# A graph network on one core: the opening of its first stage is put in another order, and its products get a wider ring of accumulators

## The chip, the cores and the metric

The kernel runs on one core of a Trainium2 chip. The metric is the device time of one execution in microseconds. It is compared by the median of several runs. The profile is that of a single further execution, so its own time stands beside its span below.

## What is computed

Four graph layers over the same 2708 nodes of 512 features, each with a residual and a layer norm. The change touches the first of them only. Cut to what matters:

```
keep    = (adj > 0) & (cumsum(adj > 0, axis=1) <= 64)     # the first 64 neighbours of a row
nb_mean = (keep @ x) / max(keep.sum(1), 1)
xj      = leaky_relu(nb_mean @ W_nb.T + b_nb)
xi      = leaky_relu(x @ W_line.T + b_line)
x       = layernorm(x + xi + where(cnt > 0, xj, 0))
# then three more layers of the form x = layernorm(x + layer(x, adj, ...))
```

The other layers are a mean over all neighbours, an attention with 8 heads, and a two-stage attention with a two-layer network behind it.

## The kernel before

The nodes are cut into 22 tiles of 128 rows (`NT`), the last of 20 rows. The features are 4 blocks of 128 (`KD`). A product of a tile with a 512 x 512 weight is four logical matmuls in float32; the trace shows each as two instructions of TensorE.

The first stage (lines 329 to 425) runs over the tiles of `x` and does three things side by side.

- **Two products per tile.** Tile `t` is fetched on SP's queue (line 175), transposed by TensorE in four pieces (line 134) into a PSUM tile `ps_tr`, and copied to `xT` by ScalarE (line 136). Then it is multiplied by `wnT` (line 397; for tiles 0 and 1 line 344) and by `wlT` (line 415). The first result is split by `keep_y` into a rounded part `yH` (ScalarE, line 241) and a rest `yL` (VectorE, line 246). The second gets its bias on VectorE, as `u` (line 417), and goes to DRAM on GpSimd's queue (line 418).
- **Counts of 14 masks** (`HERE`). A mask is 128 rows of the adjacency matrix, loaded and converted to bf16 on GpSimd's queue (line 282) into one of three tiles `m`. `count` (line 287, ScalarE) makes 0 and 1 of it and sums each row. `place` (lines 293 and 296, VectorE) marks, by a scan along the row and a product, which neighbours are among the first 64; it is done in two halves, one before and one after `u` in the program.
- **Turning of the masks.** Each is transposed into `maskT`, one way or the other. Some go through a DMA transpose on SP's queue (line 314) and are written by ScalarE two tiles later (`signs`, line 319). The others go through 22 transposes on TensorE (line 305), in three groups that take an accumulator each and are written by ScalarE (line 309).

[...]two tiles `ps_tr`, one each of `pm0` and `pm1` (pool `ps_mm`, for products with `wnT` and `wlT`), and a ring of four tiles `acc` (pool `ps_a`, handed out by `sums()`). Products with `wnT` use `acc` in odd tiles and `pm0` in even ones; products with `wlT` always use `pm1`; the groups of turned masks use `acc`.

Ahead of the loop stand the weights. `transpose_weight` (lines 139 to 148) fetches a weight in four strips, transposes each with TensorE and copies it with VectorE. In the kernel before, `wnT` is made, then tiles 0 and 1 are multiplied by it, then `wlT` is made, then the loop begins. The first two mask tiles get their zero padding from VectorE once `wlT` is done (line 354); later ones from GpSimd (line 356).

The order of the work comes from the program, from a planner that lays out each engine's queue when the kernel is built, and from ties written out by hand. `pe(...)` chains TensorE instructions in the order in which they are written. `tc.issue_after(ins)` puts what is written inside it behind `ins` on the same engine. `early(first, n, make)` makes tiles `first` steps ahead of their use. Which tile counts a mask is decided by `now` (line 406): in tile `t` one is counted if fewer than `(t - 1) * 14 / 17`, rounded up, have been.

The second stage (from line 429) multiplies the turned masks with `yH` and `yL` (line 573) and processes the other eight masks meanwhile.

Of the kernel before, what the change touches and what calls it, by code (L numbers as in the profile page):

```python
# [19 lines left out]
P = 128  # L20
D = 512
KD = D // P
# [9 lines left out]
def kernel(  # L32
# [9 lines left out]
    nc = tc.nc  # L42
    N = x.shape[0]
    NT = -(-N // P)
# [17 lines left out]
    ident = const.tile([P, P], F32, name="ident")  # L62
# [4 lines left out]
    ones = const.tile([P, P], F32, name="ones")  # L67
# [37 lines left out]
    def pe(ins):  # L105

        for i in ins.ins if isinstance(ins.ins, tuple) else (ins.ins,):
            if behind:
                tc.add_manual_dep(i, behind[0], mybir.DependencyInfo(
                    mybir.DependencyClass.NoSync, mybir.DependencyReason.DATA), reason="order")  # L110
            behind[:] = [i.name]
# [4 lines left out]
    def layer_norm(pool, y, n, dst, on_scalar=False):  # L116
# [10 lines left out]
        nc.vector.scalar_tensor_tensor(mv[:n, 0:1], mv[:n, 0:1], -1.0, rs[:n], op0=OP.mult, op1=OP.mult)  # L127
        nc.scalar.activation(dst, y, AF.Identity, bias=mv[:n, 0:1], scale=rs[:n])

    def transposed(pool, psum, src, n, name, order=as_it_comes):  # L130

        ps = psum.tile([P, KD, P], F32, name="ps_tr")
        for k in range(KD):
            order(nc.tensor.transpose(ps[:, k, :n], src[:, k * P:(k + 1) * P], ident[:n, :n]))
        dst = pool.tile([P, KD, P], F32, name=name)
        nc.scalar.copy(dst[:, :, :n], ps[:, :, :n])  # L136
        return dst

    def transpose_weight(room, psum, dst, src, queues=(nc.sync,)):

        for ki in range(KD):
            wr = room[ki]
            queues[ki % len(queues)].dma_start(wr, src[ki * P:(ki + 1) * P, :])
            ps = psum.tile([P, KD, P], F32, name="ps_tr")
            for ko in range(KD):
                pe(nc.tensor.transpose(ps[:, ko, :], wr[:, ko * P:(ko + 1) * P], ident))
            made = nc.vector.tensor_copy(dst[:, :, ki * P:(ki + 1) * P], ps)
        return made


    fast = ctx.enter_context(ExitStack())
# [55 lines left out]
    with ExitStack() as phase:  # L207
# [30 lines left out]
        highs = {}  # L238

        def keep_y(t, n, pm):  # L240
            highs[t] = nc.scalar.copy(yH(t)[:n], pm[:n])
            if t == LAST:
                low = slice(TWIN, TWIN + n)
                nc.scalar.copy(yL(t)[low], pm[low])
                return nc.vector.tensor_sub(yH(t)[low], pm[low], yL(t)[low].bitcast(F32))
            return nc.vector.tensor_sub(yL(t)[:n], pm[:n], yH(t)[:n].bitcast(F32))
# [5 lines left out]
        def product(xT, n, w, which, order=as_it_comes, pm=None):  # L252
            pm = ps_mm.tile([P, D], F32, name=f"pm{which}") if pm is None else pm
            if n == few and order is as_it_comes:
                nc.gpsimd.memset(xT[:, :, n:32], 0.0)
                for k in range(KD):
                    nc.tensor.matmul(pm[32 * k:32 * k + 32], xT[:, k, :32], w[:, k, :], start=True, stop=True)
                u = sm.tile([P, D], F32, name="u")
                nc.scalar.copy(u, pm)
                pm = sums()  # L260
                nc.tensor.matmul(pm[:TWIN + few], groups4[:, :TWIN + few], u, start=True, stop=True)
                return pm
            m = n
            if n == few:
                m = TWIN + n
                nc.gpsimd.memset(xT[:, :, n:TWIN], 0.0)
                nc.gpsimd.tensor_copy(xT[:, :, TWIN:m], xT[:, :, :n])
            for k in range(KD):
                order(nc.tensor.matmul(pm[:m], xT[:, k, :m], w[:, k, :], start=(k == 0), stop=(k == KD - 1)))  # L269
            return pm  # L270
# [58 lines left out]
        with ExitStack() as ph:  # L329
            st = ph.enter_context(tc.tile_pool(name="l0a", bufs=1))  # L330
            wnT, wlT = weight(), weight2
            room = [maskT[:, G + k, :4 * D].bitcast(F32) for k in range(2 * KD)]

            fetches = []
            xs = early(2, NT, lambda t: fetched(x, t, rows(t), log=fetches))
            xTs = early(0, NT, lambda t, order=as_it_comes: transposed(ahead, ps_tr, xs(t), rows(t), "xT", order))

            transpose_weight(room[:KD], ps_tr, wnT, l0_w_nb, (nc.sync, nc.scalar))  # L340
            lows = {}
            for t in range(2):
                xT = xTs(t, order=pe)
                lows[t] = keep_y(t, P, product(xT, P, wnT, 0, pe))
            weights_made = transpose_weight(room[KD:], ps_tr, wlT, l0_w_line)
            b_line = bias(bcast(l0_b_line, D))
            def mask_tile():
                return st.tile([P, NT * P], BF16, name="m", bufs=3)

            def mask_rows(i):  # L350
                m = mask_tile()
                if i < 2:
                    with tc.issue_after(weights_made.ins):
                        nc.vector.memset(m[:, (0 if rows(turns[i]) < P else N - 1):], 0.0)
                else:
                    nc.gpsimd.memset(m[:, N:], 0.0)
                return load_mask(i, m)

            def by_dma(i):
                return i % 2 == 0 and i < HERE - 2  # L360

            def turned_tile():
                return end_tile(BF16)[:, :NT * P].rearrange("p (t n) -> p t n", n=P)

            masks = early(1, HERE, mask_rows)
            intos = {}

            def turn_next(i):
                if not by_dma(i):
                    for _ in turn_here(i, masks(i), lambda: sums(BF16, (P, G, P)), pe):  # L370
                        pass
                    return
                assert len(intos) < 2
                intos[i] = turned_tile()
                with tc.issue_after(fetches[-1].ins):
                    turn(i, masks(i), intos[i])
                due.append((t + 2, i))

            def signs_of(i, t):
                with tc.issue_after(highs[t].ins):  # L380
                    for _ in signs(i, intos.pop(i)):
                        pass
            masks(0)
            nc.gpsimd.memset(maskT[:, NT - 1, :], 0.0)
            nc.gpsimd.memset(maskT[:, :, N:], 0.0)
            counted = turned = 0
            due, stored = [], {}
            for t in range(NT):
                n = rows(t)
                if t == END:  # L390
                    assert not due and turned >= HERE - 2
                    ends[:] = [end_tile(F32R) for _ in range(2)]
                    for y in (yH, yL):
                        nc.gpsimd.memset(y(LAST).bitcast(F32), 0.0)
                if t > 1:

                    lows[t] = keep_y(t, n, product(xTs(t, order=pe), n, wnT, 0, pe, sums() if t % 2 else None))
                xT = xTs(t)
                if t + 1 < NT:
                    xTs(t + 1, order=pe)  # L400
                while due and due[0][0] <= t:
                    signs_of(due.pop(0)[1], t)
                while turned < min(HERE, counted - (t + 2 < NT and not by_dma(turned))):
                    turn_next(turned)
                    turned += 1
                now = counted < min(HERE, -(-(t - 1) * HERE // (NT - 5)))
                if now:
                    with tc.issue_after(stored[t - 1].ins) if t > 2 else nullcontext():
                        m = masks(counted)
                    places = st.tile([P, N // 2], BF16, name="places", bufs=1)  # L410
                    with tc.issue_after(highs[t].ins):
                        count(counted, m)
                    with tc.issue_after(lows[t].ins):
                        place(counted, m, places, 0, 2)
                pm = product(xT, n, wlT, 1, pe)
                u = sm.tile([P, D], F32, name="u")
                low = nc.vector.tensor_add(u[:n], pm[:n], b_line[:n])  # L417
                stored[t] = nc.gpsimd.dma_start(r0_dram[t * P:t * P + n, :], u[:n])
                if now:
                    with tc.issue_after(low.ins):  # L420
                        place(counted, m, places, 1, 2)
                    counted += 1
            with tc.issue_after(stored[LAST].ins):
                twins(0, turns[HERE - 1] + 1)
                twins(turns[0], NT)
# [1177 lines left out]
```

## Time and profile before

| | us |
|---|---|
| median of 3 runs | 2898.84 |
| lowest and highest of them | 2898.26, 2900.93 |
| the profiled execution, its own time | 2901.17 |
| its span | 2899.3 |
| TensorE busy | 2819.1 |
| VectorE busy | 1984.4 |
| ScalarE busy | 1504.1 |
| GpSimd busy | 242.4 |

By stretches of the span (us):

| stretch | what it is | TensorE busy | VectorE busy | ScalarE busy |
|---|---|---|---|---|
| 0 to 30.6 | weights, tiles 0 and 1 | 22.0 | 11.2 | 4.1 |
| 30.6 to 193.75 | tiles 2 to 20 of the loop | 154.9 | 129.8 | 92.9 |
| 193.75 to 590 | end of the loop, second stage | 385.1 | 248.1 | 160.2 |

How such lines are read: a line of the timeline has the start, the length, the engine, the line of the kernel, the operation, output and inputs with shapes, and the number of instructions merged into it. In square brackets stands how long the engine was idle before, and whose end released it. A line of the waits has who waited for whom, the total, the times and the longest. PE is TensorE, PEld its weight loads, DVE is VectorE, ACT is ScalarE, POOL is GpSimd, SP issues transfers. The ends of matmuls are modelled, so the length of a group is a little more than the distance to the next one.

### The profile page before, as it was taken

The page shows a single profiled execution, that of the slowest core. Times are in us where ns is not written, and L with a number is a line of the kernel's source. Part 1 is how long each engine was busy: PE and PEld are TensorE (multiplying, and loading weights), DVE is VectorE, ACT ScalarE, POOL GpSimd, SP SyncE. Part 2 cuts the span into 40 slices and gives each one's busy share as a digit, 9 for nine tenths or more (in the row PEclk, how much of TensorE's full clock was granted, in tenths as well). Part 3 has the DMA queues.
Part 4 walks back from the last instruction along what each step waited for, and adds up shares of the span by engine and source line. Part 5 has one row for each costly group of instructions (what it writes and reads, how often), then busy time and mean ns, then how long its engine had stood idle before and what let it go on. Part 6 is the DMA issues. An engine that isn't in the chain of part 4 may idle for free. (4 is left out here: it accounts for less than half of the span.)

```text
span 2899.3 us, 35911 instructions
## 1 busy us (share of the span) xinstructions
PE 2819.1 (97%) x14062; PEld 1568.1 (54%) x14062; DVE 1984.4 (68%) x2343; ACT 1504.1 (52%) x1749; POOL 242.4 (8%) x395
## 2 busy tenths in 40 slices
PE   8999999999999999999999999999999999999998
PEld 4457765458887434444466433444375555555565
DVE  6867847442335999999978999999954435445342
ACT  3556632122323999999955999999951000000011
POOL 1111110101110000000022000000200010100011
PEclk9999999999999999999999999999999999999999
DMA  6845636322222011111153111110161000000000
GB/s 152 160 100 130 148 98 173 113 67 88 84 71 76 27 37 36 35 46 47 34 150 112 37 37 36 46 52 34 35 163 59 4 26 15 26 15 16 15 22 21
DMA packets 162005, 191.65 MB, mean 66 GB/s; under 512 B 82485, under 2 KB 107386, under 8 KB 161826
## 3 DMA queue, kind: packets, MB, share of 16 engines
q1 hardware_dynamic: 132342, 127.59, 15.6%
q0 software_dynamic: 18480, 57.45, 7.0%
q10 hardware_dynamic: 11004, 4.22, 0.6%
q8 instruction: 113, 1.85, 0.3%
q14 instruction: 66, 0.54, 0.1%
HBM read 148.91 MB, written 44.65 MB: 67 GB/s over the span
## 5 line engine op out<-in xcount | busy, mean ns | idle before, releaser
L830 DVE SCALAR_TENSOR_TENSOR e<-v_bc,ucol,maskT 128x1408 f32<-128x1408 f32 (+3 forms) x798 | 1131.9, 1484 | 315.3 <-PE pn L1234 307.2
L859 ACT ACTIVATE c<-e,bcol 128x1300 fp8e4<-128x1300 f32 (+2 forms) x688 | 957.9, 1414 | 60.9 <-DVE e L830 16.4
L1031 PE MATMUL po<-e,R 128*64 128x512 f32 (+3 forms) x4224 | 893.9, 548 | 25.7 <-DVE e L830 23.6
L1031 PEld LDWEIGHTS po<-e,R 128*64 128x64 f32 (+1 forms) x4224 | 334.5, 136 | 552.1 <-issue 389.6
L1234 PE MATMUL pn<-e,R 128*128 128x512 f32 (+1 forms) x1008 | 396.3, 557 | 0.8
L1234 PEld LDWEIGHTS pn<-e,R 128*128 128x128 f32 x1008 | 177.5, 190 | 195.9 <-issue 181.5
L1163 ACT ACTIVATE w<-pl,b 128x256 f32<-128x256 f32 (+1 forms) x88 | 41.1, 467 | 365.5 <-PE pl L1161 365.5
L573 PE MATMUL acc<-yH,kT 128*128 128x512 f32 x418 | 170.0, 407 | 6.7 <-ACT kT L436 4.8
L269 PE MATMUL pm<-weight,xT 128*128 128x512 f32 (+1 forms) x344 | 159.5, 607 | 10.0 <-DVE u L417 8.6
L751 PE MATMUL pm<-w,xT 128*128 128x264 f32 (+1 forms) x704 | 166.5, 390 | 1.8 <-ACT xT L136 0.9
L123 POOL TENSOR_TENSOR ln_rs<-ln_rs,half 128x1 f32<-128x1 f32 (+1 forms) x88 | 55.5, 631 | 1341.5 <-DVE ln_rs L122 1335.1
L573 PE MATMUL acc<-yL,kT 128*128 128x512 f32 x418 | 163.3, 391 | 0.0
L624 PE MATMUL acc<-yH,mf 128*128 128x512 f32 x418 | 162.7, 389 | 0.0
L624 PE MATMUL acc<-yL,mf 128*128 128x512 f32 x418 | 162.6, 389 | 0.0
L1161 PE MATMUL pl<-lin 128*128 128x256 f32 (+1 forms) x704 | 152.9, 371 | 0.6 <-DVE lin L1060 0.6
L1186 PE MATMUL pl<-lin,w 128*128 128x512 f32 x336 | 150.8, 593 | 0.0
L1161 PEld LDWEIGHTS pl<-lin 128*128 128x128 f32 x704 | 129.3, 190 | 31.2 <-issue 15.8
L751 PEld LDWEIGHTS pm<-w,xT 128*128 128x128 f32 (+1 forms) x704 | 130.8, 191 | 24.8 <-issue 1.9
L621 ACT CAST mf<-maskT 128x1024 fp32r<-128x1024 fp8e4 (+1 forms) x66 | 64.6, 979 | 151.6 <-PE acc L624 148.0
L269 PE MATMUL pm<-w,xT 128*128 128x512 f32 x296 | 133.5, 594 | 3.9 <-ACT xT L136 2.1
L436 ACT ACTIVATE kT<-maskT 128x512 fp32r<-128x512 fp8e4 (+1 forms) x132 | 77.9, 595 | 100.8 <-PE acc L573 100.6
L931 PE MATMUL pd<-c,parts_c 128*12 128x384 fp8e4 (+2 forms) x2688 | 128.3, 307 | 0.0
(268 smaller groups left out, 2684.3 us busy)
## 6 DMA issues: line engine op xcount, KB each, us to landing
rows<-x_dram SPq DMA_DIRECT2D x63, 256.0 KB
v_bc<-v_dram SPq DMA_DIRECT2D x16, 704.0 KB
rows<-in_x_dram SPq DMA_DIRECT2D x42, 256.0 KB
x_dram<-u POOLq DMA_DIRECT2D x42, 256.0 KB, 2.4
v_bc<-v_dram SPq DMA_DIRECT2D x16, 650.0 KB
m<-in_adj_dram POOLq DMA_DIRECT2D x13, 677.0 KB, 6.8
r_dram<-u POOLq DMA_DIRECT2D x21, 256.0 KB, 3.2
rows<-r_dram SPq DMA_DIRECT2D x21, 256.0 KB
```

The lines of the kernel that those rows point to most:

```text
L269: order(nc.tensor.matmul(pm[:m], xT[:, k, :m], w[:, k, :], start=(k == 0), stop=(k == KD - 1)))
L436: made = nc.scalar.activation(kT[:, :w], maskT[:, j, b[0] * P:b[0] * P + w], AF.Relu, scale=-1.0)
L573: nc.tensor.matmul(pa[t], kT[:, (t - b[0]) * P:(t - b[0] + 1) * P], y(j), start=(j == 0 and y is yH), stop=(j == LAST))
L624: nc.tensor.matmul(pa, mf[:, j - g0, :], y(j), start=(j == 0 and y is yH), stop=(j == LAST))
L751: nc.tensor.matmul(pm[a][:m, :D // 2 + heads], xT[:, k, :m], w[:, k, a, :D // 2 + heads], start=(k == 0), stop=(k == KD - 1))
L830: self.made = nc.vector.scalar_tensor_tensor(e[:, :w], v[:, :w], ucol[:, j, h:h + 1], maskT[:, j, c0:c0 + w], op0=OP.max, op1=OP.mult)
L859: nc.scalar.activation(c[:, :w], e[:, :w], AF.Sigmoid, bias=bcol[:, j, h:h + 1], scale=STEP, saturate=False)
L931: pe(nc.tensor.matmul(p[32 * g:32 * g + 12, :c1 - c0], parts_c[:, j, h, :], c[:, c0:c1], start=(i == 0 and h == hs[0]), stop=(i == NT - 1 ...
L1031: pe(nc.tensor.matmul(po[i][HO * k:HO * k + HO, :c1 - c0], R2[at, j, h * HO:(h + 1) * HO], e[at, a:a + c1 - c0], start=(i_ == 0), stop=(i_ ...
L1161: nc.tensor.matmul(pl[:, :w], self.lin1[:, k, f * P:(f + 1) * P], h[:, k, :w], start=(k == 0), stop=(k == KD - 1))
L1186: nc.tensor.matmul(pl[:n], gT[:, f, (t - t0) * P:(t - t0) * P + n], self.lin2[:, f, :], start=(f == 0), stop=(f == KF - 1))
L1234: nc.tensor.matmul(pn[k][:, :w], R2[at, j, k * P:(k + 1) * P], e[at, :w], start=(j == 0), stop=(j == NT - 1))
```

## The change

- `transpose_weight` becomes a generator: it starts all four transfers at its first step, and each step transposes and copies one strip.
- Eight products of the constant tile `ones` with itself, whose result nobody reads, are put ahead of the first weight's transposes. They take one `acc` tile.
- Two of the four strips of `wlT` are turned between tile 1's transposes and its product with `wnT`, the other two behind that product. That product goes to `acc` instead of `pm0`, and VectorE's part of its `keep_y` is put behind the last copy of `wlT`.
- The zero padding of the first three mask tiles, not two, comes from VectorE, and waits for the first copied strip of `wlT`, not for the last.
- The count in tile `t` is decided by `t * 14 / 18`, not `(t - 1) * 14 / 17`; so tile 1 has one, and tiles 5, 9 and 14 have none, where before tiles 7 and 13 had none.
- A count is also put behind the newest copy of `xT` on ScalarE.
- Products with `wlT` of even tiles go to `acc`, those of odd tiles to `pm1`.

```diff
+    copied = []
+
     def transposed(pool, psum, src, n, name, order=as_it_comes):
...
-        nc.scalar.copy(dst[:, :, :n], ps[:, :, :n])
+        copied[:] = [nc.scalar.copy(dst[:, :, :n], ps[:, :, :n])]
         return dst
 
     def transpose_weight(room, psum, dst, src, queues=(nc.sync,)):
 
         for ki in range(KD):
-            wr = room[ki]
-            queues[ki % len(queues)].dma_start(wr, src[ki * P:(ki + 1) * P, :])
+            queues[ki % len(queues)].dma_start(room[ki], src[ki * P:(ki + 1) * P, :])
+        for ki in range(KD):
             ps = psum.tile([P, KD, P], F32, name="ps_tr")
             for ko in range(KD):
-                pe(nc.tensor.transpose(ps[:, ko, :], wr[:, ko * P:(ko + 1) * P], ident))
-            made = nc.vector.tensor_copy(dst[:, :, ki * P:(ki + 1) * P], ps)
-        return made
+                pe(nc.tensor.transpose(ps[:, ko, :], room[ki][:, ko * P:(ko + 1) * P], ident))
+            yield nc.vector.tensor_copy(dst[:, :, ki * P:(ki + 1) * P], ps)
...
-            transpose_weight(room[:KD], ps_tr, wnT, l0_w_nb, (nc.sync, nc.scalar))
+            warm = sums()
+            for _ in range(8):
+                pe(nc.tensor.matmul(warm[:, :P], ones, ones, start=True, stop=True))
+            first_weights = list(transpose_weight(room[:KD], ps_tr, wnT, l0_w_nb, (nc.sync, nc.scalar)))
+            line_weights = transpose_weight(room[KD:], ps_tr, wlT, l0_w_line)
             lows = {}
-            for t in range(2):
-                xT = xTs(t, order=pe)
-                lows[t] = keep_y(t, P, product(xT, P, wnT, 0, pe))
-            weights_made = transpose_weight(room[KD:], ps_tr, wlT, l0_w_line)
+            xT = xTs(0, order=pe)
+            lows[0] = keep_y(0, P, product(xT, P, wnT, 0, pe))
+            xT = xTs(1, order=pe)
+            weights_made = [next(line_weights) for _ in range(2)][0]
+            pm = product(xT, P, wnT, 0, pe, sums())
+            with tc.issue_after(list(line_weights)[-1].ins):
+                lows[1] = keep_y(1, P, pm)
...
-                if i < 2:
+                if i < 3:
                     with tc.issue_after(weights_made.ins):
                         nc.vector.memset(m[:, (0 if rows(turns[i]) < P else N - 1):], 0.0)
...
-                now = counted < min(HERE, -(-(t - 1) * HERE // (NT - 5)))
+                now = counted < min(HERE, -(-t * HERE // (NT - 4)))
                 if now:
                     with tc.issue_after(stored[t - 1].ins) if t > 2 else nullcontext():
                         m = masks(counted)
                     places = st.tile([P, N // 2], BF16, name="places", bufs=1)
-                    with tc.issue_after(highs[t].ins):
+                    with tc.issue_after(highs[t].ins), tc.issue_after(copied[0].ins):
                         count(counted, m)
...
-                pm = product(xT, n, wlT, 1, pe)
+                pm = product(xT, n, wlT, 1, pe, None if t % 2 else sums())
```

## The prediction

> **What bounds the kernel now.** I read the page first (engines, and the wait behind each group), then the waits of TensorE over the first stage, then the timelines of TensorE and VectorE there.
>
> ```profile
> span 2899.3 us, 35911 instructions
> PE 2819.1 (97%) x14062; PEld 1568.1 (54%) x14062; DVE 1984.4 (68%) x2343; ACT 1504.1 (52%) x1749; POOL 242.4 (8%) x395
> ...
> L269 PE MATMUL pm<-weight,xT 128*128 128x512 f32 (+1 forms) x344 | 159.5, 607 | 10.0 <-DVE u L417 8.6
> ```
>
> TensorE is busy for 97% of the span, so a microsecond that it loses in the first stage is lost at the end, unless a later stage waits for something else. Cutting the trace at 193.8 us, it is busy 385.1 of the next 396.2 us and 2257.1 of the last 2309. The waits in those parts are for ScalarE or VectorE work of their own stage, not for a transfer with a fixed hour, so I carry a gain of the first stage whole to the end. The group above shows what there is to gain: the products of line 269 stood 8.6 us behind `u` of line 417, the VectorE add that empties `pm1`.
>
> ```profile
> PE pm L269 <- DVE u L417: 8.6, 7, 3.7
> PE ps_tr L146 <- DMA maskT<-in_L_gnn_W_nb_dram: 4.8, 1, 4.8
> PE pm L269 <- DVE yL L246: 1.1, 1, 1.1
> PE ps_tr L146 <- DVE weight L147: 0.9, 2, 0.5
> PE pm L269 <- DVE weight L147: 0.8, 1, 0.8
> PE pm L269 <- ACT xT L136: 0.7, 1, 0.7
> ```
>
> These are all of TensorE's waits above the view's limit in the first 200 us (total, times, longest). Seven waits make the 8.6: one of 0.35 at 27.08, then 0.98, 1.28, 0.59, 3.74, 0.44 and 1.25 in the tile loop, 8.28 together.
>
> ```profile
> 107.21 0.60 PE L134 MATMUL ps_tr<-ident,rows 128*128 128x128 f32 x4
> 111.55 6.56 PE L269 MATMUL pm<-weight,xT 128*128 128x512 f32 x8 [3.74 <-DVE u L417]
> 117.95 3.60 PE L269 MATMUL pm<-w,xT 128*128 128x512 f32 x8
> ```
>
> ```profile
> 103.90 3.03 DVE L293 TENSOR_TENSOR_SCAN places<-m,places,over 128x1354 bf16<-128x1354 bf16 x1
> 106.97 0.86 DVE L296 TENSOR_TENSOR m<-m,places 128x1354 bf16<-128x1354 bf16 x1
> 107.94 2.98 DVE L293 TENSOR_TENSOR_SCAN places<-m,over 128x1354 bf16<-128x1354 bf16 x1
> 110.83 0.67 DVE L417 TENSOR_TENSOR u<-pm,bias 128x512 f32<-128x512 f32 x1
> ```
>
> The worst one: tile 10's product ended at 103.9, but VectorE went through two scans first and read it at 110.83. The next product waited, and then took 6.56 us where its neighbour takes 3.60: the clock record has half speed from 110.51 to 117.34. So this wait cost 3.74 + 2.96 us.
>
> [...]the first transposes start 213 ns apart, after 8.15 us 109 ns apart, and the slow piece is 6.83 us[...] The pools take 2 + 2 + 4, so a product in `acc` takes a place from the ring rather than adding one. [...]
>
> **The change, part by part.**
>
> *Constant products.* Eight products of 128 columns are 16 instructions; at half clock 213 ns each, 3.4 us. `ones` is ready at 1.01, so they run from about 1.07 to 4.5, ahead of the first transposes at 4.76, which wait for a transfer: they cost nothing, and at most 0.3 if that transfer came sooner. [...] The 16 transposes gain little: the copies between them (0.69 each, two `ps_tr` buffers) and VectorE's constant work until 5.78 hold them. First copy about 5.8, fourth done about 8.4, tile 0's transposes 7.9, its copy to 9.2, product about 9.3 instead of 9.87: 0.6 us. Bounds 0 and 1.7 (an execution whose clock came later before).
>
> *Weights around tile 1's product.* After product 0 (9.3 to 12.75) come tile 1's transposes (to 13.2) and two of the second weight's. The second of these needs the buffer that tile 1's copy frees at 14.1, so product 1, now in `acc` and no longer behind `yL` at 14.92, starts at 14.6 and issues until 18.0. The last two sets follow at once (18.0 to 18.9), their copies end at 19.5 and 20.1, and line 415's first product starts at 20.15 instead of 22.60. The second one has `pm1` to itself (0.35 gone with smaller pieces), and tile 2's first product starts at 27.5 instead of 30.62: **3.1 us** for both parts. The order of transfers on SP stays; the four line-weight loads (issued 4.81 to 7.0) had landed before 15.3. `yL` of tile 1 is moved behind the last copy; who waits for it is only the ring, 20 us later.
>
> *Masks and counts.* The memsets wait for the first weight copy (14.4 instead of 22.5), and the third moves from GpSimd (0.21) to VectorE (0.15), which is idle there, except that 1.4 us of memsets may sit ahead of the second copy; product 1 covers that. The mask loads on GpSimd's queue start some 8 us earlier, and the third leaves its place behind a store of `u` (43.18, then 43.84); row transfers beside them have 20 us of room (row 4 issued at 14.04, used at 34.05), so zero. The first count follows tile 2's copy (24.6), table load and count take 1.28 + 2.65, and the first scan starts at 28.6 instead of 39.3. The new tie of a count to the row copy costs nothing: all 14 counts stand behind it on ScalarE already. So VectorE leads by 10.7 us where TensorE leads by 3.1. Work is the same: 14 masks; but they spread over tiles 1 to 17 (skipping 5, 9, 14), not 2 to 17 (skipping 7, 13).
>
> *Ring.* Line 415's products of even tiles go to `acc`, odd ones to `pm1`: each `pm1` product now waits for the `u` of two tiles back. To see which waits remain I lay both queues out by hand. TensorE: 7.31 a tile (64.20 to 71.51), 8.83 with a turned mask (71.51 to 80.34). VectorE: 8.87 a placed mask (39.32 to 48.19), with the tile's `u` after the first scan. From 27.5 and 28.6:
> - tile 4: the turn wants mask 1 at 45.9, placed at 46.2. Wait up to 0.5.
> - tiles 3, 5, 7: `pm1` wants u1, u3, u5 at about 38, 54, 70; they end at 32, 50, 64. None.
> - tile 7: the turn's third group takes the bank of u6 at 69.8; u6 ends 68.6. None.
> - tile 9: mask 5's count waits for its load (about 73) and ScalarE's signs, its scan starts at 76.2, VectorE ends it at 84.9. The turn's third group wants u8 at 86; u8 stands behind mask 6's first scan and ends at 88.6. Wait 2.6.
> - tiles 11 to 20: u9 94 against 104; mask 7 placed 108.8 against 111.3; mask 9 127.5 against 127.5; u16 152.0 against 151.9; the others looser. None above 0.2.
>
> So 3.1 us of waits stay (bounds 0 and 8). The loop loses 8.28 of waits, 2.96 of half clock and about 0.6 in restarts (a product after a wait takes 3.53, not 3.43).
>
> **Sum.** 3.1 + 8.3 + 3.0 + 0.6 = 15.0, less 3.1 = **11.9 us**. The profiled execution took 2901.17 (span 2899.3), so 2889.3 by its own time; it is 2.3 above the median of the runs, 2898.84, from which I take the gain: **2886.9**.
>
> **Rivals.** *Waits half removed (2892.3).* The program orders each engine's queue by its own planning; a scan put before a `u` moves VectorE by 3 us and keeps some of the waits. For: at 103.9 it did so. Against: the early start gives 7.6 us. It leaves 3.1 + 3.4 = 6.5 gained. *No change (2896).* Loop paced by the mask chain of load, count, placing and turning with three buffers, so only the opening's 3.1 stays; this is also the case in which the change doesn't do what it says in the loop. For: VectorE waited 13.9 us for counts. Against: TensorE's own waits name `u` alone. *Slower (2910).* One mechanism: SP's queue. A mask transpose by DMA waits there for the mask to be placed (5.8 us at 42.4), and the row fetches of four tiles ahead stand behind it. TensorE no longer waits for VectorE, so it could run into rows not fetched. By my layout the tightest row, 8, comes 7 us early. If VectorE is later than that at the five such transposes, each costs some 5 us, and [...]half of the time 3.0 more: about 26 against the 15.0 removed, 11 slower.
>
> **How the numbers follow.** Forecast 0.58 (own range 2884 to 2890.5), half removed 0.20, no change 0.14, slower 0.08. About 0.2%, 5.8 us, is what a measurement of this kernel can tell from no change. Faster by more: 0.58 and nearly all of 0.20, 0.76; within it 0.16; slower 0.08. The range runs from 2882.8 (16 gained: no wait left, opening at its best) to 2895 (4 gained), leaving out most of the no-change case and the slower one.
>
> **What would show it.** Right: 16 short products before 4.7; tile 2's first product near 27.5; no half-clock piece near 110; waits for `u` under 4 us in the loop; tile 21's first product near 182 instead of 193.75. Wrong: waits of turns for `acc`, transposes of rows waiting for a transfer, or a gain at 182 that is gone by 590.

## The result, and the profile after

| | median us | runs | lowest to highest |
|---|---|---|---|
| before | 2897.72 | 11 | 2894.48 to 2900.93 |
| after | 2892.45 | 11 | 2889.38 to 2894.67 |

The ratio is 0.998, with a 95% interval from 0.997 to 0.9989: about 5.3 us faster, where 11.9 were forecast. The time lies inside the forecast range and outside the likeliest case's own (2884 to 2890.5); it is that of the first rival, "waits half removed". The two profiled executions are further apart, 2901.17 and 2892.55, by 8.6 us. The paragraph "The executions compared" says where the other 3 come from.

From the page of the kernel after, the span, the engines and a group of line 270 (269 before; the helper grew by a line):

```profile
span 2890.8 us, 35938 instructions
PE 2816.7 (97%) x14078; PEld 1568.2 (54%) x14078; DVE 1984.9 (69%) x2344; ACT 1502.1 (52%) x1749; POOL 242.2 (8%) x394
...
L270 PE MATMUL pm<-weight,xT 128*128 128x512 f32 (+1 forms) x256 | 117.0, 600 | 0.6 <-DVE u L616 0.6
```

TensorE does the same work with 16 instructions more. The products into `pm1` no longer stand behind `u`: the 0.6 us left belong to a later stage (line 616). Half of the products with `wlT` now go to `acc` and are another group, so this line alone says nothing of their waits. The waits of TensorE in the first 200 us do (who waited for whom, total, times, longest):

```profile
PE acc L306 <- DVE u L425: 3.6, 1, 3.6
PE acc L270 <- ACT maskT L310: 1.3, 1, 1.3
PE acc L343 <- DVE ones L68: 1.1, 1, 1.1
PE acc L270 <- DVE weight L149: 0.9, 1, 0.9
PE acc L306 <- DVE m L297: 0.9, 1, 0.9
PE pm L270 <- ACT xT L138: 0.7, 1, 0.7
```

`u` is there again, at 3.6 us in one wait, with another one waiting: line 306, the turned mask, for a bank of `acc`. The loop's waits are the 3.6, 1.3 and 0.9. By TensorE's timeline they come to 3.55 + 0.89 + 1.25 = 5.7 us, where the kernel before had 8.28. Tile 9 of the loop, TensorE first (start, length, the wait in brackets):

```profile
85.35 0.72 PE L306 MATMUL acc<-identb,m 128*128 128x128 bf16 x10
86.96 0.51 PE L306 MATMUL acc<-identb,m 128*128 128x128 bf16 x6 [0.89 <-DVE m L297]
91.02 0.90 PE L306 MATMUL acc<-identb,m 128*128 128x128 bf16 x6 [3.55 <-DVE u L425]
91.86 4.96 PE L270 MATMUL pm<-weight,xT 128*128 128x512 f32 x8
```

and VectorE beside it:

```profile
86.04 0.87 DVE L297 TENSOR_TENSOR m<-m,places 128x1354 bf16<-128x1354 bf16 x1
86.82 0.69 DVE L247 TENSOR_TENSOR yL<-pm,yH 128x512 fp32r<-128x512 f32 x1
87.42 2.97 DVE L294 TENSOR_TENSOR_SCAN places<-m,over 128x1354 bf16<-128x1354 bf16 x1
90.30 0.67 DVE L425 TENSOR_TENSOR u<-acc,bias 128x512 f32<-128x512 f32 x1
```

The 22 transposes of mask 5 break after 16: their third group needs the bank in which tile 8's product stands. That product had been complete since about 81.6, but its `u` came behind a scan at 90.30. This is the same picture as at 110.83 in the kernel before, with the waiting party exchanged. The half clock came along too, from 91.01 for 3.41 us, and the product behind it took 4.96 in place of 3.60.

### The profile page after: what moved, and what is told of

Same layout as the page of the kernel before. It is cut to its first block, busy times and chain, and to the rows that moved or that the text cites. A ratio compares the mean times of both kernels' runs of the same rounds, so it can differ in the third digit from the quotient of the medians.

```text
span 2890.8 us, 35938 instructions
## 1 busy us (share of the span) xinstructions
PE 2816.7 (97%) x14078; PEld 1568.2 (54%) x14078; DVE 1984.9 (69%) x2344; ACT 1502.1 (52%) x1749; POOL 242.2 (8%) x394
## 5 line engine op out<-in xcount | busy, mean ns | idle before, releaser
L270 PE MATMUL pm<-weight,xT 128*128 128x512 f32 (+1 forms) x256 | 117.0, 600 | 0.6 <-DVE u L616 0.6
```

## The experiments

"Tile 2" and "tile 21" are the starts of these tiles' first products on TensorE, in the one profiled execution; "waits" are TensorE's in the loop, over the view's limit. Ratios are to the kernel before, by runs of it taken together with them.

| kernel | tile 2 | tile 21 | waits | half clock in the loop | median us | ratio, 95% interval |
|---|---|---|---|---|---|---|
| before | 30.62 | 193.75 | 8.3 | 6.83 | 2897.72 | |
| after | 27.65 | 186.25 | 5.7 | 3.41 | 2892.45 | 0.998, 0.997 to 0.9989 |
| opening alone | 28.43 | 189.64 | 7.5 | 3.41 | 2896.18 | 0.9987, 0.998 to 0.9994 |
| ring alone | 30.28 | 194.32 | 7.9 | 3 x 3.41 | 2902.10 | 1.0006, 0.9998 to 1.0014 |
| after, no ring | 28.22 | 186.37 | 6.5 | none | 2895.83 | 0.9987, 0.998 to 0.9993 |
| after, old counts | 26.87 | 188.48 | 7.8 | 6.83 | 2897.08 | 0.9987, 0.998 to 0.9994 |
| after, `u` first | 27.61 | 180.62 | 2.1 | none | 2890.94 | 0.9966, 0.9954 to 0.9978 |
| after, count first | 27.86 | 181.45 | 2.3 | none | 2889.11 | 0.9961, 0.9948 to 0.9975 |
| both first | 27.66 | 179.79 | 1.1 | none | 2887.47 | 0.9956, 0.9942 to 0.9969 |
| after again | 27.58 | 186.68 | 5.3 | 6.83 | 2891.71 | 0.998, 0.9972 to 0.9988 |
| after, one constant product | 30.14 | 189.31 | 5.2 | 6.83 | 2892.72 | 0.998, 0.9971 to 0.999 |
| both first again | 27.66 | 180.25 | 1.5 | none | 2884.83 | 0.9955, 0.9941 to 0.9968 |
| both first, no ring | 28.21 | 183.18 | 3.1 | none | 2887.64 | 0.9965, 0.9952 to 0.9979 |
| before again | 32.68 | 193.37 | 7.0 | 3.41 | 2906.72 (one run) | |

The medians of the kernel before were 2899.71 (opening alone to old counts), 2900.18 (`u` first to both first, and before again) and 2898.65 (after again, one constant product, both first again, both first without the ring); compare by the ratios.

My theory after the result: the opening is worth its 3 us; the ring moves the waits from the products to the turned masks, because `u` still stands behind the scans; and VectorE is late at tile 9 because ScalarE's counts come late. The rivals are named in each expectation.

### Opening alone

```diff
-                now = counted < min(HERE, -(-t * HERE // (NT - 4)))
+                now = counted < min(HERE, -(-(t - 1) * HERE // (NT - 5)))
...
-                pm = product(xT, n, wlT, 1, pe, None if t % 2 else sums())
+                pm = product(xT, n, wlT, 1, pe)
```

> The opening of the change (constant products, second weight around tile 1's product, earlier padding) with the loop of before: products with wlT in pm1 alone, counts from tile 2. My theory: the opening is worth 3 us by itself and nothing hides it, so tile 2's first product stands near 27.6 us and the time is 3 us under the kernel before; TensorE's waits for u in the loop stay as before, about 8 us. Rival, the loop is paced by the chain of masks: the lead of 3 us is eaten by longer waits for u in the loop, and the time is that of before within 1 us.

Measured: the ratio of 0.9987 is 3.8 us (1.7 to 5.8 by its interval), tile 2 starts at 28.43, not at 27.6, which is 2.2 us earlier than before, and the waits for `u` are 7.5 us in the loop, the same six as before to 0.01 us, but for the longest, 3.01 against 3.74. The opening's gain reaches the end, and the waits in the loop did not grow. The rival falls.

### Ring alone

In the kernel before:

```diff
-                pm = product(xT, n, wlT, 1, pe)
+                pm = product(xT, n, wlT, 1, pe, None if t % 2 else sums())
```

> The kernel before with one line of the change: products with wlT of even tiles go to acc. My theory: the seven waits for u go away except where a turned mask of an odd tile takes the bank of the even tile's product before it; some 4 to 6 us of the 8.3 are gained, and the half clock near 110 us with them. Rival, VectorE itself is late: the waits move from pm1 to acc, and less than 2 us are gained.

Measured: no gain, 1.0006 with one inside the interval. TensorE's waits from 30 to 190 us:

```profile
PE acc L305 <- DVE u L417: 5.9, 2, 3.4
PE acc L269 <- ACT maskT L309: 2.0, 1, 2.0
```

The six waits for `u` of line 269, 8.3 us, are gone, and 7.9 us have come in their place: two turned masks of odd tiles (5 and 17, 3.35 and 2.55) that wait for the even tile's product in the ring, and a product that waits for ScalarE to empty a turned mask. A piece at half clock came with each of the three. My 4 to 6 us were wrong; the rival's number was right. Its reason, VectorE late as such, is taken up with the `u` first kernel.

### The change without the ring, and with the old counts

The first undoes the second edit of "opening alone" only, the other the first.

> The change without the wider ring: products with wlT in pm1 alone. My theory: the opening's 3 us stay, and the earlier counts give VectorE a lead of 7 us that pm1 cannot use in full, since its product waits for the u of the tile before: waits for u of 4 to 8 us, time 2 to 4 us over the changed kernel. Rival, the ring costs as much as it gives, by the turned masks that wait for it: time equal to the changed kernel or under it.

> The change with the old formula for the counts (from tile 2). My theory: VectorE is a tile later, so the turned masks of odd tiles wait longer for acc: 3 to 5 us more of waits than in the changed kernel and a time 2 to 4 us over it. Rival, the earlier counts don't matter, because VectorE then waits for later masks: time within 1 us of the changed kernel.

Measured: both 0.9987, the same as the opening alone. Their medians are 2895.83 and 2897.08 beside 2899.71, so each of them gained 2.6 to 3.9 us, and the changed kernel, with 0.998, some 2 us more. The times agree with my theory, but the intervals overlap with that of the changed kernel, so by time alone it is not settled. The waits are those I named without the ring (six for `u`, 6.5 us); with the old counts they are 5.9 for `u` and 1.9 for ScalarE, 2.1 more than in the changed kernel and not 3 to 5. Of the 8.3 us of waits before, the opening alone takes 0.7 off, the opening with the earlier counts 1.8, the opening with the ring 0.5, all three 2.6; the ring in the kernel before takes off 0.3.

One number speaks for the rival: in its profiled execution the kernel without the ring reached tile 21 at 186.37, as early as the changed kernel (186.25), since its waits, none over 1.89 us, brought no half clock. What the ring is worth in the changed kernel is not shown.

### `u` first

```diff
-                    with tc.issue_after(lows[t].ins):
-                        place(counted, m, places, 0, 2)
...
                     with tc.issue_after(low.ins):
+                        place(counted, m, places, 0, 2)
                         place(counted, m, places, 1, 2)
```

> The changed kernel with both halves of a tile's placing written behind its u on VectorE, so that u no longer stands behind the first scan. My theory: the wait of 3.55 us at tile 9 is for a bank of the ring that u8 empties only behind a scan; u8 now comes about 3 us sooner, at 88, the wait falls to about 1 us or less and the half clock behind it goes: 2 to 4 us under the changed kernel. Rival, VectorE as a whole is late: the wait moves to the placed mask (turned mask of line 306 behind line 297), and less than 1 us is gained.

Measured: 0.9966, so 4 us beyond the changed kernel's ratio; the intervals of the two overlap (0.9954 to 0.9978, 0.997 to 0.9989), and it is the trace that says why. The same place on VectorE:

```profile
85.33 0.69 DVE L423 TENSOR_TENSOR u<-acc,bias 128x512 f32<-128x512 f32 x1
85.93 2.97 DVE L294 TENSOR_TENSOR_SCAN places<-m,over 128x1354 bf16<-128x1354 bf16 x1
```

`u` of tile 8 now comes at 85.33 instead of 90.30, ahead of the first scan of mask 6. Both waits of tile 9 are gone, and no half clock came in the loop. The rival, a VectorE with too much work, falls: it does the same work here. One wait is left, 2.1 us at tile 13, for ScalarE's line 310.

The edit did more than I had named. I expected `u` of tile 8 some 3 us sooner, which is the scan that stood ahead of it; it came 5.0 us sooner. The load of a mask is tied behind the store of a tile's `u`, so one of them was issued at 48.02 instead of 51.32. The signs of mask 2 found their transpose done, so that the count of mask 4 ended sooner and its placing began sooner; that the transpose was done because of the earlier load is likely and not shown:

```profile
62.52 2.83 ACT L320 ACTIVATE maskT<-end 128x1024 fp8e4<-128x1024 bf16 x4
67.92 2.98 DVE L294 TENSOR_TENSOR_SCAN places<-m,over 128x1354 bf16<-128x1354 bf16 x1 [1.91 <-ACT m L288]
```

The changed kernel has these two at 64.82 and 70.22 (next section). So this run takes away a part of the late count too. By my estimate from the changed kernel's trace, the order alone would put `u` at 87.4, where the scan stood, with its end near 88.1, and leave a wait of some 0.6 us at tile 9 in place of 3.55.

### The count first

```diff
-                while due and due[0][0] <= t:
-                    signs_of(due.pop(0)[1], t)
...
-                        count(counted, m)
+                        got = count(counted, m)
...
+                while due and due[0][0] <= t:
+                    with tc.issue_after(got.ins) if now else nullcontext():
+                        signs_of(due.pop(0)[1], t)
                 pm = product(xT, n, wlT, 1, pe, None if t % 2 else sums())
```

(`count` returns its instruction.) Its reason lies in the changed kernel's ScalarE at tile 6,

```profile
62.16 0.59 ACT L138 COPY xT<-ps_tr 128x512 f32<-128x512 f32 x1
64.82 2.83 ACT L320 ACTIVATE maskT<-end 128x1024 fp8e4<-128x1024 bf16 x4 [2.07 <-DMA end<-m]
67.56 2.54 ACT L288 ACTIVATE m<-m,gate 128x2708 bf16<-128x2708 bf16 x1
```

and in VectorE behind it:

```profile
65.55 0.69 DVE L425 TENSOR_TENSOR u<-acc,bias 128x512 f32<-128x512 f32 x1
70.22 2.98 DVE L294 TENSOR_TENSOR_SCAN places<-m,over 128x1354 bf16<-128x1354 bf16 x1 [3.98 <-ACT m L288]
```

The signs of mask 2 wait 2.07 us for its DMA transpose and take 2.83; the count of mask 4 stands behind them, and VectorE idles for 3.98 us.

> The changed kernel with ScalarE's signs of a DMA-turned mask written behind the tile's count, not ahead of it. My theory: VectorE lost 3.98 us at 66.2 to 70.2, because count 4 stood behind the signs of mask 2, which waited for their transpose until 64.8; with the count first its scan starts near 65.5, u8 comes some 4 us sooner, the wait at tile 9 is under 1 us: 2 to 4 us under the changed kernel. Rival, the chain of mask loads sets the counts: VectorE's idle time only moves to the next counts, and less than 1 us is gained.

Measured: 0.9961, 5.5 us beyond the changed kernel's ratio where I had named 2 to 4; its interval, too, overlaps that of the changed kernel. From VectorE and TensorE:

```profile
65.74 2.97 DVE L294 TENSOR_TENSOR_SCAN places<-m,over 128x1354 bf16<-128x1354 bf16 x1
87.30 0.67 DVE L426 TENSOR_TENSOR u<-acc,bias 128x512 f32<-128x512 f32 x1
88.02 0.59 PE L306 MATMUL acc<-identb,m 128*128 128x128 bf16 x6 [1.39 <-DVE u L426]
```

The scan that started at 70.22 starts at 65.74, `u` of tile 8 at 87.30 instead of 90.30 (3.0 us sooner, not 4), and the wait of tile 9 is 1.39, a little over the 1 us that I named. VectorE's later idle time grew by 1.08 at 75.57, as the rival has it, but only by a quarter of what was gained.

### Both, and again on one chip with the changed kernel

> Both edits together. My theory: no wait of TensorE over 1 us is left in the loop, and no half clock there: 4 to 6 us under the changed kernel, about 2887 where the kernel before has 2897.7. Rival: under 2 us gained, since VectorE's work of 8.87 us a placed mask is what holds the loop.

> The version with u ahead of the placing and the count ahead of the signs, again, on one chip with the changed kernel. My theory: 4 to 6 us under the changed kernel. Rival: less than 2 us.

> The changed kernel as it is, beside the others on one chip. My theory: the waits of its profile (0.9 and 3.6 at tile 9, 1.2 at tile 13) come again within 0.2 us; the half clock behind the second need not; 5 to 6 us under the kernel before. Rival: its gain on the first measurement was chance of the clock, and is under 3 us here.

Measured: 0.9956 and 0.9955, against 0.998 of the changed kernel, whose waits came back as 3.55, 0.85 and 0.81; the last had been 1.25, so it did not come within 0.2 us. The half clock came with the 3.55 again. On one chip the medians are 2884.83 and 2891.71: 6.9 us, a little over what I expected, and every run of the version (2883.68 to 2885.75) is under every run of the changed kernel (from 2890.3). Of the loop's waits one over 1 us is left, where I expected none; in the first of the two profiles it is

```profile
PE acc L270 <- ACT maskT L310: 1.1, 1, 1.1
```

and in the second 1.3, with one of 0.2 for ScalarE's copy of `xT`. This version beats both kernels. What it gains over the changed one at tile 21, 6.5 us (186.25 to 179.79), is the 4.6 of waits and the half clock.

### Both first, without the ring

> The same version without the wider ring: products with wlT in pm1 alone. My theory: with u ahead of the scans it mostly ends within the 3.9 us that the next product leaves it, so only some of the waits for u come back, 1 to 4 us in all, and the time is 1 to 4 us over the version with the ring. Rival: the ring is worth nothing once u is first; the time is the same within 1 us.

Measured: 2887.64 beside 2884.83, 2.8 us over, with three waits for `u` of 3.1 us. The ring is worth that once `u` doesn't stand behind scans, and nothing by itself in the kernel before. The two intervals of the ratios overlap (0.9952 to 0.9979, 0.9941 to 0.9968), but these hold the spread of the kernel before as well; the runs themselves don't overlap (2886.02 to 2890.38 without the ring, 2883.68 to 2885.75 with it, five each, on one chip).

### One constant product, and the kernel before again

```diff
-            for _ in range(8):
+            for _ in range(1):
                 pe(nc.tensor.matmul(warm[:, :P], ones, ones, start=True, stop=True))
```

> The changed kernel with one constant product in place of eight. My theory: the clock comes up [...]at 8 to 14 us, the first transposes and part of the first products run at half speed: tile 2's first product 0.5 to 2.5 us later, time 0.5 to 2.5 us over the changed kernel. Rival: the copies between the transposes set the pace and nothing changes, within 0.3 us.

> The kernel before, for another profile of it. My theory: the waits for u come again, within 0.1 us each, but the piece at half clock near 110 us [...]it need not come[...], and the time is then 1 to 3 us under the first profiled execution (2901.17). Rival: the 6.8 us at half clock come with the wait of 3.7 us each time.

The opening with one constant product (in the changed kernel the first line is `1.06 3.78 ... x16`):

```profile
1.06 0.80 PE L343 MATMUL acc<-ones 128*128 128x128 f32 x2 [1.06 <-DVE ones L68]
4.75 3.84 PE L148 MATMUL ps_tr<-ident,maskT 128*128 128x128 f32 x16 [2.90 <-DMA maskT<-in_L_gnn_W_nb_dram]
8.53 1.12 PE L136 MATMUL ps_tr<-ident,rows 128*128 128x128 f32 x4
10.32 5.34 PE L270 MATMUL pm<-w,xT 128*128 128x512 f32 x8 [0.68 <-ACT xT L138]
```

Here the clock came up at 13.66, so that tile 0's first product took 5.34 us in place of 3.70, and tile 2 started at 30.14, 2.5 us later. In the median of the runs the difference is 1.0 us (2892.72 to 2891.71), less than the intervals resolve. So eight products in place of one are worth 2.5 us in that execution, and how much on average is not settled.

The kernel before, again: five of the six waits came as before to 0.01 us, the longest was 2.47 and not 3.74 (7.0 us in all), and the half clock with it lasted 3.41 us, not 6.83. So its length is not fixed; but I was wrong on the time: with the clock up at 13.74 only and four pieces at half clock (112.7, 225.4, 1478 and 1553) that execution took 2906.72, one of the longest of this kernel.

## Why the prediction was half right

**Opening, 3.1 us: right.** Tile 2's first product started at 27.65 (forecast 27.5), the first scan at 29.05 (28.6). Alone it is worth 3.8 us by the ratio, with 1.7 to 5.8 in the interval. The 0.6 us of the constant products in it was my estimate: tile 0's product started at 9.46 in place of 9.87, 0.41 us sooner, with the clock up at 5.68 in place of 8.11. Their bounds, 0 to 1.7, were too narrow: 2.5 against one product, in one execution.

**The gain carries to the end: right.** At tile 21 the profiles were 7.5 us apart, at the first product of line 632 (624 before; 620.32 and 627.20) 6.9, and 8.5 in the span. The last step holds luck: the kernel before had a piece at half clock at 1496 us, which this execution of the kernel after had not.

**"So 3.1 us of waits stay (bounds 0 and 8)": this term failed.** It was 5.7. The mechanism was named and the place too: "tile 9: ... The turn's third group wants u8 at 86; u8 stands behind mask 6's first scan and ends at 88.6. Wait 2.6." In the trace it ended at 90.97, and the waits there were 0.89 + 3.55. The same line had mask 5's scan start at 76.2; it started at 78.60, because mask 4 was placed only then. The layout had left out one step there: in tile 6 ScalarE has the signs of mask 2 ahead of the count of mask 4, and these wait for a transfer, so the count ended at 70.2. The kernel with the count first shows it: this one edit takes the wait to 1.39. The kernel with `u` first shows the other half: no wait is left at tile 9 though VectorE's work is the same, if with some help from an earlier count. Of the prediction's own signs, tile 21's first product came at 186.25 and not near 182, and the sign of being wrong that it named first, a turn waiting for `acc`, is the one that came. The 1.25 at tile 13 I had not seen: a count of ScalarE, released at 117.90, stood ahead of the emptying of a turned mask, whose bank the next product needed. What released that count so late is named by the trace as the placing of the mask before; a kernel without this wait wasn't tried, so its cause stays open.

**"The loop loses 8.28 of waits, 2.96 of half clock": the second number belongs to one execution.** The kernel after brought its own half clock, 3.41 us in one profile and 6.83 in the other, the kernel before 6.83 and 3.41. It came with each wait of 3 us or more, in all the kernels, and its length differed between executions with the same wait; the last section has the waits and the records of the clock. So it must not be booked as removed as long as such a wait is left. Without it and with the waits as measured the sum reads 3.1 + 8.3 + 0.6 - 5.7 = 6.3, and the runs gave 5.3 and 6.9.

**The executions compared.** The profiled execution of the kernel before was on the long side of its runs (2901.17 where the median is 2897.72). I moved to the median for the level, but took the gain from that execution alone: 8.6 between the profiles is 5.3 between the medians.

**The rivals.** "Waits half removed (2892.3)" is what happened, and in part by its reason: a scan ahead of a `u` kept the longest wait. It was no new scan, though: `u` of tile 8 stood behind one in the kernel before as well (90.5 behind 87.6), and what made it cost 3.55 us was that mask 4 was late and that a turned mask now waited for the bank. That the time agrees to 0.2 us is luck: the rival gained 6.5 us from 2898.84, the kernel 5.3 from 2897.72. The slow rival did not come: no transpose of rows in the loop waited for a fetch. Its sum doesn't come out either: five transposes at 5 us and half of 3.0 are 32.5, not 26.

## What to carry to other kernels

When a product gets another accumulator, ask what else lives in that ring: the wait for a late reader moves to the ring's next user, and here came back at nearly its old size. The cure was on the reader's engine: put the short instruction that frees the bank ahead of the long ones, and work that is ready ahead of work that waits for a transfer; 13 to 14 us for both with the rest of the change, against 5 to 7 without. Half clock came here with every wait of 3.01 us or more, so a gain from the clock is not safe while such a wait is left, and an estimate from one execution should leave it out.

## What the runs showed of the hardware

- Waits of TensorE in the loop of 3.01 us (opening alone), 3.35 (ring alone, and after with old counts), 3.55 (the three profiles of the changed kernel with eight constant products or one) and 3.74 (before) each came with half clock for 3.41 or 6.83 us. Of those between 2 and 2.6 us, 2.04 and 2.55 (ring alone) and 2.47 (before again) did, 2.08 (`u` first) and 2.56 (old counts) did not; none of 1.89 or less.
- In the clock records of the first profile of the kernel before and of the kernel after, all changes of an execution lie whole multiples of 3.413 us apart. In the kernel after the clock was up at 5.68, down at 91.01 and up at 94.42, steps of 25 and 1 times 3.413; in the kernel before it was up at 8.11, down at 110.51, up at 117.34, down at 1496.32 and up at 1499.73, steps of 30, 2, 404 and 1. In the last 3.413 us ahead of the fall in the loop TensorE had been idle, by its modelled ends, for all 3.41 us in the kernel after and for 2.70 in the kernel before; counted in the same steps from where the clock came up, in no other one at full clock in their first 200 us had it been idle for more than 1.28. Later that doesn't sort them: ahead of the fall at 1496.32 it was 1.92, and 1.92 in the kernel after from 1483.7 on, with no fall. The piece of 6.83 us had TensorE idle for 1.04 us in its first half, that of 3.41 us for 0.01.
- The clock came up at 4.1 to 7.3 us in the ten profiles with eight constant products (after: 5.68), and at 8.1, 9.8, 13.7 and 13.7 in the four without (before: 8.11, one constant product: 13.66, before again: 13.74). The first transposes of the kernel before started 213 ns apart ahead of 8.11, 109 ns apart behind it. A product of a tile, 3.70 us at full clock behind a wait, took 5.34 where the clock came up within it (one constant product), and 6.56 in the kernel before, nearly all of it at half clock.
- The signs of a mask in the changed kernel's tile 6 waited for a DMA transpose that was issued at 55.60 and released them at 64.82, behind a mask load issued at 51.32 whose packets ran until about 57; the first transpose, issued at 37.87 with no mask load under way, freed its mask by 43.29.
